# Context halves of batch 0 added by DMA, and the last denominators of a batch copied out of PSUM before they are inverted

## The chip, the cores and the metric

The kernel runs on one core of a Trainium2 chip as one launch. The time is the device time of that core in microseconds. A core has five engines that run their own instruction streams and meet at semaphores: TensorE (PE in the profile, with its weight loads as PEld), VectorE (DVE), ScalarE (ACT), GpSimd (POOL) and SyncE (SP), which here only issues DMAs. [...]

## The reference

Two layers over an fp32 tensor x of 4 batches, 1024 channels and 32 x 32 positions. The change lies in the first, an attention over the N = 1024 positions of each batch:

```python
qkv = (x @ w_qkv.T + b_qkv).reshape(B, N, 3, nh, hd)   # 16 heads of 64
q, k = rmsnorm(rope(q)), rmsnorm(rope(k))
attn = softmax(einsum('bqhd,bkhd->bhqk', q, k) * hd ** -0.5)
ctx  = einsum('bhqk,bkhd->bqhd', attn, v).reshape(B, N, inner)
out  = rmsnorm(ctx @ w_proj.T) + x
```

The second layer is a bottleneck of three convolutions (1x1, 3x3, 1x1) with batch norms, a residual and relu. It is not touched.

## The kernel before, in words

**Stages.** The four batches are worked one after the other: projections of q, k and v, attention, output projection; then the second layer for all batches. The projections are block products of the Strassen kind, in two levels of 7 products each (`OUTER` has the order; `project2` issues them): a PE product of 8 matmuls goes into one PSUM bank, and VectorE, ScalarE and GpSimd make the sums of operands before it and of results after it. The sums of the weights' blocks don't depend on the batch. They are made once, in batch 0: `prepare` (L386-397) and `prepare_blocks` (L399-414) load four blocks, let VectorE make four sums of 128x512 (L392-395), and let GpSimd write them to DRAM (L397, L414), from where later products read them.

A second copy of the program, with shifted scores, stands behind a branch that these inputs don't take.

**Attention.** Each batch has two query halves (`c`, 512 queries each) and eight pairs of heads (`hp`); one step of the two loops is called a head here, 16 a batch. A head has

- eight key tiles `t`: score matmuls for two heads of 64 and two halves of the keys into an `sc` tile (two PSUM banks; three such tiles), L787; the exponential by ScalarE from there into SBUF, 128x1024, L794; and the running sum of the exponentials on VectorE, the denominators `d_` (L798, L800);
- 64 context matmuls (L807) with the values as weights, the lower half of the keys into `o[:, 0]`, the upper half into `o[:, 1]`. `o` is the tile `cx`, of which PSUM has one (two banks);
- the halves' sum: ScalarE copies `o[:, 0]` into its place in `q_all` (L812), and VectorE adds `o[:, 1]` to it (L836). Between the two in VectorE's stream stand what lies in the code between L812 and L835: the multiplication of earlier contexts by their inverse denominators (`mean_of_v`, L764, with GpSimd's bias after it, L765), the inversion of earlier denominators, and in batch 0 one or two weight steps (`extra`: 21 in all).

After every second head, matmuls with ones (L846) sum the denominators over partitions into `dn`, an `sc` tile. In batches 1 to 3 this holds for the second query half alone; the denominators of the first go through `halve` and `sum_of_eight`. What is to be done with `dn` is put on the list `late` and taken from there at the start of the next head, or, for the last one of a batch, 0.1 products into the output projection. That is the function `inverses`: it copies `dn` to SBUF (L900), sends it through DRAM into a small tile `few` of 128x16 (`to_few`, L881-888), inverts it there (L904), sends it back and lets `spread` load it over the partitions (L914). The last `dn` of a batch is treated in another way: VectorE inverts it straight from PSUM, 128x512 (L896), and `spread` copies from SBUF.

**Pools.** `temp` gives tiles of 128x512 in SBUF, four in turn; the weight sets of `prepare` take four each of the eight tiles of `wring`. Attention's PSUM (`sc` 3 x 2 banks, `cx` 1 x 2) and the projections' (`o1` and `o2`, 4 banks each) are the same eight banks: `psum_for` closes the one pools and opens the others, so a projection's first products wait until what lay in their banks has been read.

**Order.** The streams of PE, GpSimd, VectorE and ScalarE follow the code's order here (`manual_schedule`); SP's DMAs are ordered by the framework's scheduler. During a projection `after(n, step)` puts a step n products later; `waiting` holds work that is slipped in when there is room. At the end of a batch's attention the output projection starts with products of q's blocks, while `after(0.1)` issues the last inversion, `after(1)` and `after(4)` the sums of context blocks (L281-284), and `after(3)` the last `mean_of_v`. `load_parts` issues the loads of the next weight set, at the fourth key tile of a head.

Of the kernel before, what the change touches and what calls it, by code (L numbers as in the profile page):

```python
# [13 lines left out]
ALU = mybir.AluOpType  # L14
# [9 lines left out]
NHP = C // (2 * HD)  # L24
CH = 512
NCH = N // CH
# [37 lines left out]
QH = P // 4  # L64
# [21 lines left out]
def program(ctx, tc, x, wblk, w2, w3, vecs, cos, sin, out, bad):  # L86


    nc = tc.nc
# [63 lines left out]
    dens = dram.tile([P, CH], F32, name=f"dens{u}")  # L153
# [4 lines left out]
    with tc.tile_pool(name=f"st{u}", bufs=2) as st, ExitStack() as s:  # L158
# [44 lines left out]
        def bank(kind, name):  # L203
            pool, shape = psum[kind]
            return pool.tile(shape, F32, tag=kind, name=name)

        def temp(name):
            return tmp.tile([P, CH], F32, tag="tmp", name=name)
# [58 lines left out]
        def next_waiting():  # L267
            cost, step = waiting.popleft()
            spend(cost)
            step()  # L270
# [471 lines left out]
        def shifts(q_all, k_all, n, hp, c):  # L742

            rows = []
            for j in range(2):
                d = slice(j * HD, (j + 1) * HD)
                row = temp(f"row_{n}_{j}")[0:1, :]
                for t in range(CH // P):
                    sc = bank("sc", f"sm_{n}_{j}_{t}")
                    q = q_all[d, hp, c * CH + t * P : c * CH + (t + 1) * P]  # L750
                    for kh in range(N // CH):
                        nc.tensor.matmul(sc[:, kh], q, k_all[d, hp, half[kh]], start=True, stop=True)
                    m = acc.tile([P, 1], F32, tag="m", name=f"m_{n}_{j}_{t}")
                    nc.vector.tensor_reduce(m, sc.rearrange("p a k -> p (a k)"), AX.X, ALU.max, negate=True)
                    o = bank("sc", f"mt_{n}_{j}_{t}")[:, 0]
                    nc.tensor.matmul(o[0:1, :P], m, ident, start=True, stop=True)
                    nc.vector.tensor_copy(row[:, t * P : (t + 1) * P], o[0:1, :P])
                rows.append(row)
            return rows
# [7 lines left out]
        def attention(b, c, q_all, k_all, v, probs_, late, ready, extra, slow, steps_in_all, load_parts, fold):  # L767


            at = half[c]  # L770
            sums_, contexts = [], []
            for hp in range(NHP):
                n = f"{b}_{c}_{hp}"
                if late:
                    late.pop(0)()
                rows = shifts(q_all, k_all, n, hp, c) if bad is None else None
                probs = []
                if fold and hp % 2 == 0:
                    d_ = fold[hp // 4][:, hp % 4 // 2 * 2 : hp % 4 // 2 * 2 + 2, :]
                else:  # L780
                    d_ = acc.tile([P, 2, CH], F32, tag="tot", name=f"den_{n}")
                for t in range(N // P):
                    p = probs_[:, t]
                    sc = bank("sc", f"sc_{n}_{t}")
                    for keys in (low, high):
                        for j, d in enumerate((low, high)):
                            nc.tensor.matmul(  # L787
                                sc[keys, j], k_all[d, hp, t * P + keys.start : t * P + keys.stop], q_all[d, hp, at],
                                start=True, stop=bad is not None,
                            )  # L790
                    if bad is None:
                        for j in range(2):
                            nc.tensor.matmul(sc[:, j], ones[0:1, :], rows[j], start=False, stop=True)
                    nc.scalar.activation(p, sc, AF.Exp)  # L794
                    if t == 3:
                        load_parts()
                    if t == 1:
                        nc.vector.tensor_tensor(d_, probs[0], p, ALU.add)  # L798
                    elif t > 1:
                        nc.vector.tensor_tensor(d_, d_, p, ALU.add)  # L800
                    probs.append(p)
                o = bank("cx", f"cx_{n}")
                for t in range(N // P):
                    for j in range(2):
                        h0 = (2 * hp + j) * HD
                        for i, keys in enumerate((low, high)):
                            nc.tensor.matmul(  # L807
                                o[j * HD : (j + 1) * HD, i], v[keys, t, h0 : h0 + HD], probs[t][keys, j],
                                start=(t == 0), stop=(t == N // P - 1),
                            )  # L810

                nc.scalar.copy(q_all[:, hp, at], o[:, 0])  # L812
                contexts.append((q_all[:, hp, at], o[:, 1]))
                sums_.append(d_)
                if hp % 2 == 1:
                    for r in ready:
                        mean_of_v(q_all, *r)
                    ready.clear()
                if fold:
                    halve(hp, d_, fold[hp // 4][:, hp % 4 // 2 * 2 : hp % 4 // 2 * 2 + 2, :])  # L820
                    if hp % 4 == 3:
                        eights.append((hp + 2, lambda n=n, hp=hp: sum_of_eight(b, n, hp, fold[hp // 4], ready)))
                if half_done and half_done[0][0] <= c * NHP + hp:
                    half_done.pop(0)[1]()
                if slow:
                    slow.pop(0)()

                if waiting:
                    next_waiting()
                slots = NCH * NHP - 1  # L830
                if extra and steps_in_all == 0 and hp > 0:
                    extra.pop(0)()
                for _ in range(len(extra) - -(-steps_in_all * max(slots - 1 - c * NHP - hp, 0) // slots) if steps_in_all else 0):
                    extra.pop(0)()
                for cx, other in contexts:  # L835
                    nc.vector.tensor_tensor(cx, cx, other, ALU.add)  # L836
                contexts.clear()
                if eights and eights[0][0] <= c * NHP + hp:
                    eights.pop(0)[1]()
                if hp % 2 == 0 or fold:  # L840
                    continue
                dn = bank("sc", f"dn_{n}")[:, 0]
                for i, d_ in enumerate(sums_):
                    for j in range(2):
                        q = slice((2 * i + j) * QH, (2 * i + j + 1) * QH)
                        nc.tensor.matmul(dn[q, :], ones[:, :QH], d_[:, j], start=True, stop=True)  # L846
                sums_ = []
                late.append(lambda *a, n=n, hp=hp, dn=dn: inverses(b, c, hp, n, dn, ready))

        half_done, eights = [], []  # L850
# [39 lines left out]
        def inverses(b, c, hp, n, dn, ready):  # L890


            r = temp(f"rec_{n}")
            k = 2 * ((b * NCH + c) * NHP + hp - 1)
            if (c, hp) == (NCH - 1, NHP - 1):
                nc.vector.reciprocal(r, dn)  # L896
                nc.sync.dma_start(dens[k : k + 4, :], r[::QH, :])
                spread(c, hp, n, ready, [r[q * QH : (q + 1) * QH, :] for q in range(4)])
                return
            nc.scalar.copy(r, dn)  # L900
            few, rows = to_few(n, k, 4, r[::QH, :])

            def invert():
                nc.vector.reciprocal(few, few)  # L904
                nc.sync.dma_start(rows, few)
                spread(c, hp, n, ready, [dens[k + q, :].partition_broadcast(QH) for q in range(4)])

            half_done.append((0, invert))

        def spread(c, hp, n, ready, rows):  # L910
            w = big_temp(f"inv_{n}")
            for i in range(2):
                for j in range(4):
                    nc.sync.dma_start(w[j * QH : (j + 1) * QH, half[i]], rows[2 * i + j // 2])  # L914
                ready.append((c, hp - 1 + i, w[:, half[i]]))
# [253 lines left out]
        for b in range(B):  # L1169
            units = units_of(room)  # L1170
            q_all = kv.tile([P, NT, N], F32, tag="q", name=f"q_{b}")
# [43 lines left out]
            def load_parts():  # L1215

                while todo and len(made) < 2:
                    made.append(todo.pop(0)(pieces, nc.sync))
# [3 lines left out]
            late, ready, steps_in_all = [], [], len(extra)  # L1222
# [275 lines left out]
        for b in range(B):  # L1498
# [34 lines left out]
            if b == 0 and bad is not None:  # L1533
                o = ps.tile([P, CH], F32, tag="mm", name="fit")
# [20 lines left out]
        for f in range(NT):  # L1555
# [8 lines left out]
            for i, k in order:  # L1564
                b, c = divmod(i, NCH)
# [14 lines left out]
            sc, sh = norms[f] = norm_of(stats, col("g3", f), col("be3", f), f"3_{f}")  # L1580
# [81 lines left out]
```

## Time and profile before

| | |
|---|---|
| time, median of 3 runs | 2700.87 us (2698.98 to 2702.51) |
| profiled execution | 2704.24 us, span 2702.4 us, clock 0.992 |
| busy: PE, DVE, ACT, POOL | 98%, 80%, 41%, 17% of the span |
| attention of batch 0 | 288.3 to 542.2 us |
| its exponentials, L794 | 1.044 us each |
| its denominators, L800 and L798 | 1.225 and 1.217 us each |
| its halves' adds, L836 | 16 of 0.68 us |
| its copies of a half, L812 | 16 of 0.586 us |
| inversions of `few`, L904 | 7 of 0.25 us |
| weight stores by GpSimd, L397 | 68, of 0.55 us to issue each |

A line of the timeline gives start and length in us, the engine, the line, the operation with the tile written and those read, and the count; in brackets the idle time before it and who ended it. Consecutive instructions of one kind are merged. A line of the waits says "engine tile line <- releaser: us in total, times, longest". The stretches are in us from the span's start. A DMA on "SPq" or "POOLq" is shown where it is issued.

### The profile page before, as it was taken

The numbers are of one execution on the slowest core, as the hardware profiler recorded it, in microseconds if no ns is written. First come the engines' busy times: TensorE is split into PE (matmuls) and PEld (weight loads), VectorE is DVE, ScalarE is ACT, GpSimd is POOL, SyncE is SP. The second block draws the span as 40 slices with busy tenths as digits, with TensorE's granted clock in tenths as the row PEclk, the third lists the DMA queues.
The fourth block names the chain that finished last, engine by engine and source line by source line (L and its number), as shares of the span: only waits on it lengthen the run. The fifth ranks groups of instructions, "written<-read, shape, count | busy, mean of one in ns | idle before, by whom it ended". The sixth has DMA issues, their size and how long they took to land. (4 is left out here: it accounts for less than half of the span.)

```text
span 2702.4 us, 40776 instructions
## 1 busy us (share of the span) xinstructions
PE 2642.7 (98%) x15434; PEld 1634.4 (60%) x15434; DVE 2152.2 (80%) x2602; ACT 1112.0 (41%) x1549; POOL 470.0 (17%) x573
## 2 busy tenths in 40 slices
PE   9999998989999999999999999999999999999997
PEld 4448432378888433488887333788884334846843
DVE  5668987988887876887888777788878779877987
ACT  2222454523343565333343556233435554312266
POOL 2542233311011121200011222100111222010000
PEclk9999999999999999999999999999999999999999
DMA  7887665666677453357676441565774443493165
GB/s 274 291 249 220 199 221 190 214 204 194 207 199 207 101 96 70 124 152 222 174 196 175 91 80 41 187 190 181 199 205 106 80 103 121 141 275 123 63 226 210
DMA packets 255661, 459.76 MB, mean 170 GB/s; under 512 B 34912, under 2 KB 127632, under 8 KB 255456
## 3 DMA queue, kind: packets, MB, share of 16 engines
q1 hardware_dynamic: 210528, 306.73, 36.0%
q0 software_dynamic: 44928, 150.33, 22.1%
q8 instruction: 125, 2.05, 0.3%
q14 instruction: 80, 0.66, 0.1%
HBM read 327.43 MB, written 97.01 MB: 157 GB/s over the span
## 5 line engine op out<-in xcount | busy, mean ns | idle before, releaser
L794 ACT ACTIVATE p<-sc 128x1024 f32<-128x1024 f32 x512 | 476.1, 1044 | 18.3 <-PE sc L787 18.2
L787 PE MATMUL sc<-q,k 64*64 64x512 f32 x4096 | 453.1, 591 | 0.0
L800 DVE TENSOR_TENSOR den<-den,p 128x1024 f32<-128x1024 f32 x312 | 385.6, 1236 | 32.9 <-ACT p L794 0.5
L807 PE MATMUL cx<-p,to 64*64 64x512 f32 x3072 | 338.2, 589 | 0.0
L787 PEld LDWEIGHTS sc<-q,k 64*64 64x64 f32 x4096 | 151.0, 132 | 291.7 <-ACT p L794 143.5
L807 PEld LDWEIGHTS cx<-p,to 64*64 64x64 f32 x3072 | 117.4, 133 | 212.2 <-issue 211.9
L485 PE MATMUL p_y<-q,w_y 128*128 128x256 f32 x928 | 217.2, 388 | 21.6 <-issue 21.6
L485 PEld LDWEIGHTS p_y<-q,w_y 128*128 128x128 f32 x928 | 180.3, 195 | 51.3 <-issue 26.1
L480 PE MATMUL p_v<-w_v,x 128*128 128x256 f32 x928 | 210.0, 379 | 0.3 <-DVE x L451 0.2
L765 POOL TENSOR_SCALAR q<-q,vec 128x512 f32<-128x512 f32 x64 | 126.7, 1989 | 393.2 <-DVE q L764 393.2
L480 PEld LDWEIGHTS p_v<-w_v,x 128*128 128x128 f32 x928 | 176.1, 190 | 25.6 <-DVE x L451 1.3
L812 ACT COPY q<-cx 128x512 f32<-128x512 f32 x64 | 37.5, 586 | 362.5 <-PE cx L807 362.5
L485 PE MATMUL p_q<-to,w_q 128*128 128x256 f32 x672 | 152.2, 379 | 0.0
L485 PE MATMUL p_k<-to,w_k 128*128 128x256 f32 x672 | 152.2, 379 | 0.0
L485 PEld LDWEIGHTS p_q<-to,w_q 128*128 128x128 f32 x672 | 127.4, 190 | 18.4 <-issue 1.2
L485 PEld LDWEIGHTS p_k<-to,w_k 128*128 128x128 f32 x672 | 127.4, 190 | 18.4 <-issue 1.2
L807 PE MATMUL cx<-p,rq 64*64 64x512 f32 x1024 | 117.7, 610 | 9.3 <-DVE q L836 9.3
L1566 PE MATMUL c<-h,w 128*128 128x512 f32 x256 | 110.3, 592 | 0.5 <-ACT h L1469 0.5
L798 DVE TENSOR_TENSOR den<-p 128x1024 f32<-128x1024 f32 x52 | 63.5, 1222 | 50.8 <-ACT p L794 50.8
L800 DVE TENSOR_TENSOR den_T<-den_T,p 128x1024 f32<-128x1024 f32 x72 | 88.2, 1225 | 7.9 <-ACT p L794 0.5
L727 POOL DMA_DIRECT2D k<-ks x64 | 57.9, 1096 | 192.4 <-ACT p L794 71.1
L807 PEld LDWEIGHTS cx<-p,rq 64*64 64x64 f32 x1024 | 39.5, 137 | 85.8 <-issue 69.9
(491 smaller groups left out, 4371.7 us busy)
## 6 DMA issues: line engine op xcount, KB each, us to landing
w_v<-wd2f SPq DMA_DIRECT2D x112, 256.0 KB
w_y<-wd2f SPq DMA_DIRECT2D x112, 256.0 KB
w_q<-wd2f SPq DMA_DIRECT2D x84, 256.0 KB
w_k<-wd2f SPq DMA_DIRECT2D x84, 256.0 KB
wd2f<-w_pre POOLq DMA_DIRECT2D x68, 256.0 KB, 4.1
x<-in_x_dram SPq DMA_DIRECT2D x64, 256.0 KB
q<-qs POOLq DMA_DIRECT2D x64, 256.0 KB, 5.5
k<-ks POOLq DMA_DIRECT2D x64, 256.0 KB, 4.5
```

What stands on the lines that cost most here:

```text
L480: nc.tensor.matmul(o[:, q].rearrange("p (g f) -> p g f", g=2), r[:, i, q * P : (q + 1) * P], wt[:, :, i, :], skip_group_check=True, **at,)
L485: nc.tensor.matmul(o[:, q], wt[:, q, i, :], r[:, i, :], skip_group_check=True, **at)
L727: nc.gpsimd.dma_start(dst[i::2, f, :], other[1 - i :: 2, :], accum_op=ALU.add)
L765: nc.gpsimd.tensor_scalar(cx, cx, col("bv", hp), None, ALU.add)
L787: nc.tensor.matmul(sc[keys, j], k_all[d, hp, t * P + keys.start : t * P + keys.stop], q_all[d, hp, at], start=True, stop=bad is not None,)
L794: nc.scalar.activation(p, sc, AF.Exp)
L798: nc.vector.tensor_tensor(d_, probs[0], p, ALU.add)
L800: nc.vector.tensor_tensor(d_, d_, p, ALU.add)
L807: nc.tensor.matmul(o[j * HD : (j + 1) * HD, i], v[keys, t, h0 : h0 + HD], probs[t][keys, j], start=(t == 0), stop=(t == N // P - 1),)
L812: nc.scalar.copy(q_all[:, hp, at], o[:, 0])
L1566: nc.tensor.matmul(os[i], w3t[k][f // NH][:, f % NH, :], h2[b, k][:, half[c]], start=(k == 0), stop=(k == NPT - 1),)
```

## The change

In batch 0, for every head but the last, ScalarE copies both halves out of PSUM, the second into a temporary tile, and GpSimd issues a DMA that adds the one to the other in SBUF (256 KB). The other heads keep VectorE's add, at the same place. For the last denominators of each batch, ScalarE copies `dn` into a temporary tile right after its matmuls; at the place where the inversion was, VectorE inverts the copy in place, and the two transfers after it are the same. In batch 0 one `sc` tile is skipped before the last `dn`.

```diff
@@ attention @@
-                nc.scalar.copy(q_all[:, hp, at], o[:, 0])
-                contexts.append((q_all[:, hp, at], o[:, 1]))
+                cx = q_all[:, hp, at]
+                nc.scalar.copy(cx, o[:, 0])
+                if b == 0 and (c, hp) != (NCH - 1, NHP - 1):
+                    other = temp(f"cx_{n}")
+                    nc.scalar.copy(other, o[:, 1])
+                    nc.gpsimd.dma_start(cx, other, accum_op=ALU.add)
+                else:
+                    contexts.append((cx, o[:, 1]))
...
-                for cx, other in contexts:
-                    nc.vector.tensor_tensor(cx, cx, other, ALU.add)
-                contexts.clear()
+                if contexts:
+                    nc.vector.tensor_tensor(contexts[0][0], *contexts.pop(0), ALU.add)
...
+                if (b, c, hp) == (0, NCH - 1, NHP - 1):
+                    bank("sc", f"skip_{n}")
                 dn = bank("sc", f"dn_{n}")[:, 0]
...
+                if (c, hp) == (NCH - 1, NHP - 1):
+                    r = temp(f"rec_{n}")
+                    nc.scalar.copy(r, dn)
+                    late.append(lambda n=n, hp=hp, r=r: last_inverses(b, c, hp, n, r, ready))
+                    continue
                 late.append(lambda *a, n=n, hp=hp, dn=dn: inverses(b, c, hp, n, dn, ready))
@@ inverses @@
-            if (c, hp) == (NCH - 1, NHP - 1):
-                nc.vector.reciprocal(r, dn)
-                nc.sync.dma_start(dens[k : k + 4, :], r[::QH, :])
-                spread(c, hp, n, ready, [r[q * QH : (q + 1) * QH, :] for q in range(4)])
-                return
             nc.scalar.copy(r, dn)
@@ new @@
+        def last_inverses(b, c, hp, n, r, ready):
+            k = 2 * ((b * NCH + c) * NHP + hp - 1)
+            nc.vector.reciprocal(r, r)
+            nc.sync.dma_start(dens[k : k + 4, :], r[::QH, :])
+            spread(c, hp, n, ready, [r[q * QH : (q + 1) * QH, :] for q in range(4)])
```

## The prediction

> **What bounds the kernel now.** First the page's busy shares:
>
> ```profile
> PE 2642.7 (98%) x15434; PEld 1634.4 (60%) x15434; DVE 2152.2 (80%) x2602; ACT 1112.0 (41%) x1549; POOL 470.0 (17%) x573
> ```
>
> TensorE is the bound over the whole span, so only what shortens a stretch in which TensorE stands still, or runs at a lower clock, can pay. Two places belong to the change: batch 0's attention and the end of each batch's attention. The busy times by stretch (length, then each engine's busy time, clock, DMA share, GB/s):
>
> ```profile
> 288.30:542.20 253.90, 240.46 (x2113) 79.38 (x2112) 222.89 (x239) 133.83 (x152) 77.44 (x106) 0.98 0.63 202
> 1126.60:1130.00 3.40, 3.33 (x8) 2.74 (x9) 3.29 (x3) 0.00 (x0) 0.00 (x0) 0.51 0.73 245
> ```
>
> In the first stretch (batch 0's 16 heads) PE is idle for 13.4 us and VectorE is 88% busy; batches 1 to 3 take 13.73 us a head here with PE 100% busy, so 16 heads would be 220. The second is one outer product after a boundary, at clock 0.51. The view of waits, from 285 to 545, says who PE waits for in batch 0:
>
> ```profile
> DVE few L904 <- DMA few<-densf: 17.9, 7, 5.7
> PEld cx L807 <- DVE q L836: 15.7, 8, 5.3
> PE cx L807 <- DVE q L836: 9.3, 4, 4.4
> PEld dn L846 <- DVE den L800: 8.3, 6, 1.9
> PE dn L846 <- DVE den L800: 4.1, 4, 1.0
> ```
>
> PE waits 9.3 us for the add of the halves (it frees the one context slot in PSUM) and 4.1 us for denominators: both say that VectorE is late. VectorE itself waits 17.9 us, and only for the little tile of denominators. The timeline of one pair shows why:
>
> ```profile
> 409.23 0.59 ACT L900 COPY rec<-dn 128x512 f32<-128x512 f32 x1 [0.63 <-PE dn L846]
> ...
> 415.42 5.64 SPq L383 DMA_DIRECT2D w_pre<-in_wblk_dram  x4
> ...
> 421.16 1.99 SPq L383 DMA_DIRECT2D w_pre<-wdf  x4
> ...
> 423.25 0.50 SPq L883 DMA_DIRECT2D densf<-rec  x1
> ...
> 427.84 0.34 SPq L887 DMA_DIRECT2D few<-densf  x1
> ...
> 430.93 0.25 DVE L904 RECIPROCAL few<-few 128x16 f32<-128x16 f32 x1 [5.72 <-DMA few<-densf]
> ...
> 433.82 0.68 DVE L836 TENSOR_TENSOR q<-q,cx 128x512 f32<-128x512 f32 x1
> ...
> 434.56 10.01 PE L807 MATMUL cx<-p,rq 64*64 64x512 f32 x64 [4.45 <-DVE q L836]
> ```
>
> The denominators are in SBUF at 409.8, but their store leaves at 423.25, behind eight weight loads in SP's queue, which wait for VectorE to free their slots. VectorE idles 5.7 us at L904, then does a weight step and only then L836; PE loses 4.45 us and its context then takes 10.01 us instead of 7.1, because the clock has fallen. Last, the boundary of batch 1:
>
> ```profile
> 1120.02 1.99 PE L485 MATMUL p_y<-q,w_y 128*128 128x256 f32 x8
> ...
> 1123.22 3.35 DVE L896 RECIPROCAL rec<-dn 128x512 f32<-128x512 f32 x1
> ...
> 1126.67 3.58 PE L485 MATMUL p_y<-q,w_y 128*128 128x256 f32 x8 [4.67 <-issue]
> ...
> 1130.09 3.62 PE L485 MATMUL p_y<-y,w_y 128*128 128x256 f32 x16
> ```
>
> The second output product starts 0.1 us after VectorE's reciprocal ends: its PSUM bank lies where `dn` was, and the reciprocal reads `dn` there. It stalls 4.67 us, then takes 3.4 where others take 1.73. The other boundaries look alike; in batch 0 the last `dn` ends at 542.19, the reciprocal at 549.18, the first two products start at 549.27 and the third at 554.69.
>
> [...] here L393 takes 0.98 while L765 runs beside it and 0.69 otherwise[...]
>
> **The change, part by part.**
>
> *Boundaries, four times.* The product that waited for the reciprocal now waits for a 128x512 copy by ScalarE (0.59, as L900). The bank is free at about `dn`'s end + 0.13 + 0.6, with 0.1 to start.
> Batch 0: start at 543.1 (542.19 + 0.9), two products at full clock, third product at 543.1 + 2 x 1.73 = 546.55 instead of 554.69: 8.1. Its sums of q end on VectorE at 545.83, in time.
> Batch 1: the second product follows the first at 1121.75, the third starts at 1123.47 instead of 1130.09: 6.6; its sums end at 1123.3, just in time. Batches 2 and 3 have the same pattern: 6.6 and 6.9. Sum 28.2.
> VectorE's order is kept: the reciprocal still starts at 1123.22 and stays 3.35. So PE is now ahead of VectorE by the gain. Next late in batch 1: VectorE's adds end at 1131.25, then L506, the next sums at about 1134.4, then L764 (1135.7), POOL's L765 pair (4.1, to about 1139.5) and L282, which a product at about 1142.7 needs: some 2 us to spare. If this cover is gone, up to 3 us a boundary go back, 12 in all.
> SP's order at the boundary also moves: two loads of w_y ahead, seven x loads instead of ten up front. Each load issues in about 0.5; the weights that come earlier are needed sooner than the x loads. I take nothing, bounds -2 to +2.
>
> *Batch 0's halves.* 15 adds of 0.68 leave VectorE: 10.2 us. The context slot is freed by two ACT copies, the second 0.59 after the first, so it no longer waits behind a weight step (2.8) and an inverse. ScalarE gains 15 x 0.59 = 8.8 on 134 busy in 254: hidden, except where its copies delay the first exponential of the next head. In odd heads this sits 0.27 after the copy, so it comes about 0.3 later: 8 x 0.3 = 2.4.
> POOL gets 15 issues. The nearest row is the accumulating k<-ks of L727: 1.1 mean to issue, 4.5 to land; the store of a weight block takes 0.55. I take 1.0, bounds 0.55 and 1.8. POOL is 30% busy there (77.4 of 254), so 15 us fit, but the issue stands ahead of that head's L765 and weight stores and waits itself for ACT's copy. They leave 1 to 2.5 us later (ACT's second copy would end at 445.8 in the pair above, where L765 now starts at 444.40; then the issue). Queued behind them: the next weight set, loaded only after a store, and VectorE's step for it. Before, a set whose stores left by 354.4 had its loads issued by 359.2 and was used at 366.6; with a landing like the stores' 4.1 that leaves some 3 us of slack. The data move of 256 KB lands by estimate within 5.5 (the q<-qs row); its reader, L764, comes a pair later, about 28 us. Hidden; without this cover it would be 5 a pair.
> SP's order changes most (the framework's scheduler sets it, and it comes out differently): the store and reload of each pair's denominators stand ahead of the four or eight weight loads. `few` then lands some 5 to 8 us after the pair's end, and VectorE asks for it 12 or more after: most of the 17.9 goes.
>
> *The sum in batch 0.* Pairs started at 288.3, 319.3, 348.3, 380.3, 409.1, 445.5, 480.0 and 511.0, with `dn`'s end at 542.2: 28.9 to 36.4 each. Unstalled, a pair is 6.92 + 6.87 + 6.87 + 6.97 for its matmuls and 1.0 for `dn`, 28.6. Walking VectorE along (9.12 for a head's denominators, 2.8 a weight step, 1.3 an L764 pair, no L836, no wait for `few`), it is at most 5 us behind PE, at which no `dn` waits: 29.0 a pair with the 0.3 for ACT. Batch 0 would end at 521.5 instead of 542.2: 20.7. For weight sets that land late in heads 4, 8 and 10, I take off 2: 18.5.
> Bounds: if the wait for `few` stays, only the 10.2 of VectorE and the slot's wait help, about 9; without late sets, 20.7.
>
> 28.2 + 18.5 = 46.7. Span 2702.4 - 46.7 = 2655.7; that execution took 2704.24 (1.84 around the span), so 2657.5; it lies 3.4 over the median of 2700.87, which gives 2654.2.
>
> **Rivals.**
> *The weight chain takes over (chance 0.2).* POOL's later stores delay loads, VectorE waits for sets instead of `few`; attention gains 0 to 9. For: weight loads are at VectorE's head of queue, and now stand behind the denominators on SP. Against: the 3 us of slack. 2654 + 9.5 to 18.5 gives 2664 to 2673.
> *The boundary gives part back (0.1).* VectorE's remaining reciprocal becomes late for the sums or L764: 12 back, 2666.
> *Slower (0.07).* The accumulating DMA heads POOL's in-order queue, waits for the context's end there, and holds L765 and four weight stores until then. If stores leave 7.6 us later in each of 15 heads, 3.3 are slack and 4.3 reach VectorE and then PE: 15 x 4.3 = 65 against 46.7 gained, so 2719. It decides from some 6.4 us of delay a head (15 x 3.1 = 46.7). Against: the worst I find is the 2.5 above.
> *Nothing gained at the boundary (0.01).* If the product's real wait is on something that ended with the reciprocal by chance, 28.2 is missing: 2682; four boundaries with the same 0.1 us after it speak against. This also is where no change could come from, with the second rival's zero.
>
> **How the numbers follow.** Both parts hold: 0.62, 2654, its own range 2649 to 2662 (a microsecond or two at each boundary, up to 5 of late sets). With the two rivals of 2664 to 2673 at 0.3, the range for 8 in 10 is 2646 to 2676: the low end is the 2.2 taken off for late sets, the 2 at SP's boundaries and the 3.5 by which the runs shown spread (2654.2 - 7.7). 0.2%, 5.4 us, is about what a measurement can tell from no change: faster 0.92, same 0.01, slower 0.07.
>
> **What would show it.** Right: no idle PE over 1 us after the boundaries, the product after them at 1.7 to 1.9; no `L904` wait over 1 us; no PE wait for VectorE in `cx`; batch 0's heads at 14.5 us; accumulating DMAs landing in 3 to 6. Wrong: waits of VectorE for w_pre or of POOL for ACT's second copy, heads of over 15 us, PE waits on L764 or L765 in the output projection, or a reciprocal still just ahead of a product.

## The result and the profile after

The changed kernel takes 2666.45 us (median of 4 runs, 2663.41 to 2667.97) against 2701.69 of the kernel before beside it: ratio 0.9869, 95% interval 0.9851 to 0.9886. That is 35.2 us less, where 46.7 were forecast; the time lies inside the forecast's range, above the likeliest case's own. Measured once more later, beside another 11 runs of the kernel before, it was 2663.83 (0.9853, 0.984 to 0.9865).

The page's busy shares of the changed kernel, and the busy times of batch 0's attention (length, PE, PEld, DVE, ACT, POOL with their counts, clock, DMA share, GB/s):

```profile
PE 2630.3 (99%) x15434; PEld 1627.9 (61%) x15434; DVE 2144.5 (80%) x2587; ACT 1121.1 (42%) x1568; POOL 480.9 (18%) x588
...
289.00:525.60 236.60, 234.11 (x2113) 77.82 (x2112) 215.82 (x225) 140.21 (x167) 87.59 (x121) 1.00 0.76 229
```

The attention of batch 0 has shrunk from 253.9 to 236.6 us; VectorE is busy 7.1 us less, and PE is idle for 2.5 us instead of 13.4. Its waits over the whole span, from the view of waits (us in total, times, longest):

```profile
PE p_y L485 <- DMA w_y<-wdf: 4.5, 4, 2.3
PE dn L853 <- DVE den L800: 2.5, 4, 1.0
PE p_q L485 <- DMA w_q<-wdf: 2.1, 1, 2.1
...
PE p_v L480 <- DMA w_v<-wdf: 1.4, 1, 1.4
PE p_v L480 <- DVE x L451: 1.3, 2, 1.0
```

The kernel before has this line in the same view, for the four stalls after the attentions:

```profile
PE p_y L485 <- issue: 21.6, 4, 7.1
```

These 21.6 us are gone (0.7 is left), and so is the 9.3 us for the context slot. New is the first line of the changed kernel's: each output projection waits once for weights. The pair of batch 0 that answers to the one shown of before, in the timeline:

```profile
408.13 0.50 SPq L895 DMA_DIRECT2D densf<-rec  x1
...
410.37 0.34 SPq L899 DMA_DIRECT2D few<-densf  x1
...
415.80 4.30 SPq L383 DMA_DIRECT2D w_pre<-in_wblk_dram  x4
...
422.25 0.25 DVE L911 RECIPROCAL few<-few 128x16 f32<-128x16 f32 x1
...
422.79 0.90 POOL L817 DMA_DIRECT2D q<-cx  x1 [6.39 <-ACT cx L816]
...
428.04 7.05 PE L807 MATMUL cx<-p,rq 64*64 64x512 f32 x64
```

The store of the denominators now leaves at 408.13, ahead of the weight loads instead of behind them; VectorE inverts `few` without waiting, and the context runs at full clock (1.00 over its 7.05 us, against 0.71 over the 10.01 us of the kernel before). The boundary of batch 1, in the timeline:

```profile
1098.22 1.06 PE L853 MATMUL dn<-den,ones 128*32 128x512 f32 x8
1099.22 3.72 PE L485 MATMUL p_y<-q,w_y 128*128 128x256 f32 x16
1102.42 3.35 DVE L919 RECIPROCAL rec<-rec 128x512 f32<-128x512 f32 x1
1102.78 3.62 PE L485 MATMUL p_y<-y,w_y 128*128 128x256 f32 x16
1105.80 0.51 SPq L920 DMA_DIRECT2D densf<-rec  x1
1106.35 5.00 SPq L927 DMA_DIRECT2D inv<-rec  x8
1111.45 2.59 SPq L472 DMA_DIRECT2D w_y<-wd2f  x3
...
1114.61 0.93 SPq L383 DMA_DIRECT2D w_y<-wdf  x2
...
1119.35 1.99 PE L485 MATMUL p_y<-to,w_y 128*128 128x256 f32 x8 [0.87 <-DMA w_y<-wdf]
```

The second product no longer waits for the reciprocal, and runs at full clock (1.00 from 1099.22 to 1106.00). But SP's queue stands still from 1103.77 until the reciprocal ends at 1105.77, then spends 5 us on eight copies, and only then issues the weights. They arrive 0.87 us late.

Laying the two timelines side by side, matmul by matmul (the start of each in the one less that in the other), gives the whole account. PE's lead grows by 16.55 us up to batch 0's last `dn` (17.3 of it within the attention, which began 0.8 later). The boundaries of batches 0 to 3 bring 8.24, 6.52, 7.93 and 6.78, together 29.5. Given back are 0.80, 1.04, 0.84 and 2.51 at the first product with `to` of each, 5.2 in all, then 3.2 in batch 1's q projection, 1.3 in batch 2's v projection and 0.2 elsewhere. 16.55 + 29.5 - 5.2 - 3.2 - 1.3 - 0.2 = 36.2, and the spans differ by 36.2. (The expectations below were written with 29.2 and 5.0 for the second and the third of these.)

### The profile page after: what moved, and what is told of

Its sections match the earlier page's. It is cut to its first block, busy times and chain, and to the rows that moved or that the text cites. A ratio compares the mean times of both kernels' runs of the same rounds, so it can differ in the third digit from the quotient of the medians.

```text
span 2666.2 us, 40828 instructions
## 1 busy us (share of the span) xinstructions
PE 2630.3 (99%) x15434; PEld 1627.9 (61%) x15434; DVE 2144.5 (80%) x2587; ACT 1121.1 (42%) x1568; POOL 480.9 (18%) x588
## 5 line engine op out<-in xcount | busy, mean ns | idle before, releaser
L485 PE MATMUL p_y<-q,w_y 128*128 128x256 f32 x928 | 209.8, 379 | 0.7 <-issue 0.7
L485 PE MATMUL p_y<-to,w_y 128*128 128x256 f32 x384 | 90.5, 380 | 4.5 <-DMA w_y<-wdf 4.5
L480 PE MATMUL p_v<-w_v,t 128*128 128x256 f32 x384 | 90.1, 379 | 1.4 <-DMA w_v<-wdf 1.4
```

The source lines that it names most:

```text
L480: nc.tensor.matmul(o[:, q].rearrange("p (g f) -> p g f", g=2), r[:, i, q * P : (q + 1) * P], wt[:, :, i, :], skip_group_check=True, **at,)
L485: nc.tensor.matmul(o[:, q], wt[:, q, i, :], r[:, i, :], skip_group_check=True, **at)
```

## The experiments

**The two parts alone.** First the last denominators without the halves, VectorE adding from PSUM as before:

```diff
-                if b == 0 and (c, hp) != (NCH - 1, NHP - 1):
-                    other = temp(f"cx_{n}")
-                    nc.scalar.copy(other, o[:, 1])
-                    nc.gpsimd.dma_start(cx, other, accum_op=ALU.add)
-                else:
-                    contexts.append((cx, o[:, 1]))
+                contexts.append((cx, o[:, 1]))
```

> Only the last denominators are changed, batch 0's halves are added by VectorE as before. Theory (the two parts add up; at the boundary the bank comes free with ScalarE's copy): batch 0's attention stays at 254 us from its first score to the last dn; the stalls of 4.7 to 7.1 us after each dn are gone and 29 us are gained there; the waits for w_y of 0.6 to 2.4 us at the first product with to, 5.0 us in all, are there as in the changed kernel. Time 2701.7 - 29.2 + 5.0 = 2677.5, or 2682 if the later waits in batch 1's q and batch 2's v projection (4.4 us) also come from this part. Rival (the boundaries' gain needs the shorter attention, or its order of loads): under 15 us gained, 2687 or more.

Measured: 2676.51 against 2700.98, ratio 0.9904 (0.9888 to 0.9921): 24.5 us. Three boundaries bring what they brought together; batch 0's brings 6.6 instead of 8.2, because its first products ran at a lower clock (0.57 from 538.4 to 541.5). The wait for w_y is there (2.6 us, three times). Batch 0's attention took 250.6 us in this trace; its code and the order of SP's issues are those of before there, so 250.6 and 253.9 show that this stage can vary by 3 us between executions.

Then the halves without the last denominators (the last `dn` inverted from PSUM):

```diff
+            if (c, hp) == (NCH - 1, NHP - 1):
+                nc.vector.reciprocal(r, dn)
+                nc.sync.dma_start(dens[k : k + 4, :], r[::QH, :])
+                spread(c, hp, n, ready, [r[q * QH : (q + 1) * QH, :] for q in range(4)])
+                return
...
```

> Only batch 0's halves are changed; the last denominators are inverted from PSUM as before. Theory: batch 0's attention takes 236 to 238 us instead of 254, the four boundaries stall as before, no wait for w_y in them: 2701.7 - 17.3 = 2684.4. Rival (the attention's gain is given back where PE arrives earlier): 2690 or more.

Measured: 2689.37, ratio 0.9949 (0.9933 to 0.9966): 11.6 us, less than the 17.3 expected, with an attention of 238.2 and the four stalls as before. The 17.3 was read between two traces, and the one of before ran 3.4 us over its kernel's median. 24.5 + 11.6 = 36.1 against 35.2 for both: the parts add up.

**Which half of the halves?** Using the DMA also changed SP's order. So the kernel before got that order and nothing else:

```diff
+                with tc.manual_schedule(engines={mybir.EngineType.SP if b == 0 else mybir.EngineType.PE}):
                 attention(
...
```

> The kernel before with one thing changed: in batch 0's attention SP's transfers go in the order in which they are written, which puts the store and reload of each pair's denominators ahead of the next weight loads, as in the changed kernel; nothing else moves. Theory (the wait for few is a large part of VectorE's lag): VectorE's 17.9 us of waiting for few fall below 3, batch 0's attention takes 242 to 247 us: 2690 to 2695. Rival (VectorE's load by the adds, and the slot in PSUM that they hold, are what counts): attention 251 to 254, time 2699 to 2702.

Measured: 2687.72, ratio 0.9947 (0.993 to 0.9963): 13.3 us, no less than the DMAs with the order brought. The attention took 235.7 us, better than the theory's 242 to 247. Its waits of PE, from 285 to 530, are one line; VectorE waits for no `few`:

```profile
PE dn L846 <- DVE den L800: 1.0, 1, 1.0
```

VectorE still does all 16 adds from PSUM here. The opposite test is the changed kernel with the old order, the denominators' transfers behind the weight loads:

```diff
                     if t == 3:
                         load_parts()
+                        while sends:
+                            sends.pop(0)()
...
-            few, rows = to_few(n, k, 4, r[::QH, :])
+            sends.append(lambda: sent.append(to_few(n, k, 4, r[::QH, :])))
...
```

> The changed kernel with the store and reload of each pair's denominators behind the weight loads again, in SP's order of the kernel before. Theory (the wait for few counts): VectorE waits 10 us or more for few, batch 0's attention takes 242 to 248 us instead of 236.6, time 2672 to 2678. Rival (the adds count alone): attention within 2 us of 236.6, time 2666 to 2669.

Measured: 2678.55, ratio 0.9908 (0.9891 to 0.9925), just beyond the theory's end. The attention took 253.1 us, more than its 248, and the time is 2.0 above that of the first run, which has SP's old order too but no DMAs: without the order the DMAs gain nothing. From its views of waits of PE and of VectorE, 285 to 545, and its timeline:

```profile
PE dn L855 <- DVE den L802: 12.7, 6, 6.5
```

```profile
DVE few L917 <- DMA few<-densf: 20.3, 6, 8.2
```

```profile
432.42 0.25 DVE L917 RECIPROCAL few<-few 128x16 f32<-128x16 f32 x1 [8.16 <-DMA few<-densf]
...
444.56 1.92 PE L855 MATMUL dn<-den,ones 128*32 128x512 f32 x4 [6.54 <-DVE den L802]
```

The context no longer waits for VectorE, since ScalarE frees the slot. But VectorE idles 8.16 us for `few`, the next head's denominators are late too, and PE now loses 12.7 us at `dn` where it lost 9.3 at `cx` and 4.1 at `dn`. And the time that the adds freed on VectorE became idle time: it is busy for 215.0 of these 253.1 us, idle for 38.1 where it was idle for 31.0 before. Of the 7.1 more, 2.4 are waits for `few` (20.3 instead of 17.9), 3.0 for exponentials and 1.3 for weight sets.

Last, the changed kernel without its DMAs, in its SP order (the edit of the first run and that of the third together; in the traces SP's issues from 286 to 545 follow one another as in the changed kernel, transfer by transfer):

> The changed kernel without its accumulating DMAs: VectorE adds the halves from PSUM as in the kernel before, while SP's transfers stand in exactly the order of the changed kernel. New theory (the attention's gain is SP's order alone): batch 0's attention 235 to 238 us, time 2664 to 2669. The prediction's reading (VectorE's 15 adds and the slot they held are part of the gain): 241 to 246 us, 2671 to 2677.

Measured: 2664.42, ratio 0.986 (0.9844 to 0.9877), attention 236.4 us:

```profile
289.60:526.00 236.40, 235.17 (x2113) 78.89 (x2112) 222.48 (x240) 133.83 (x152) 77.37 (x106) 1.00 0.68 217
```

VectorE is busy 222.5 us here against 215.8 in the changed kernel, and the stage is no longer: PE is idle 1.2 us in it. Once more, with the changed kernel beside it in five rounds:

> The changed kernel once more, on the same chip as the run beside it: 2664 to 2668.

> The changed kernel without its accumulating DMAs and in its SP order, once more beside it. Theory (the DMAs add nothing to the gain): within 3 us of the changed kernel, on either side. Rival (they bring part of the 10.2 us of VectorE's adds): 4 us or more above it.

The changed kernel took 2663.83 (0.9853, 0.984 to 0.9865), the one without DMAs 2662.34 (0.9849, 0.9836 to 0.9862). They can't be told apart: the median without the DMAs was the lower one, by 1.5 us here and by 2.0 between 2664.42 and the first 2666.45, where the rival wanted it 4 us higher.

So four kernels, all with the last denominators changed, differ in these two things alone: in SP's old order 2676.51 without the DMAs and 2678.55 with them, in the new order 2664.42 and 2666.45. The order is worth 12.1 us either way. The 2.0 us that the DMAs seem to cost is inside the intervals. The trace of the changed kernel has a sign of such a cost: VectorE waits for weight sets, from the view of waits between 285 and 530,

```profile
DVE w_pre L392 <- DMA w_pre<-in_wblk_dram: 4.4, 2, 2.2
...
DVE w_pre L392 <- DMA w_pre<-wdf: 1.0, 2, 0.7
```

against 0.7 us without the DMAs. Whether the sets are late because GpSimd issues and stores later, or because the DMA share is 0.76 instead of 0.68, was not separated.

**The skipped tile.** The changed kernel without it:

```diff
-                if (b, c, hp) == (0, NCH - 1, NHP - 1):
-                    bank("sc", f"skip_{n}")
```

> The changed kernel without the skipped sc tile ahead of batch 0's last dn. Theory: dn then lies under other banks of the output projection, but a copy of 0.6 us frees it before the second product asks for it, as in batches 1 to 3: the first product starts 0.1 to 0.2 us after dn instead of 0.73, time within 1 us of the changed kernel. Rival: the bank is one that the first product needs, and the wait of 0.7 stays or grows to 2.

One execution: 2667.19, and the first product waits 0.73 us with and without it. The theory of the wait missed; the tile makes no difference that one execution can show.

**What holds w_y back.** The reading from the timeline was SP's queue. So the eight copies and the store went to ScalarE's queue:

```diff
-            nc.sync.dma_start(dens[k : k + 4, :], r[::QH, :])
-            spread(c, hp, n, ready, [r[q * QH : (q + 1) * QH, :] for q in range(4)])
+            def send():
+                spread(c, hp, n, ready, [r[q * QH : (q + 1) * QH, :] for q in range(4)], nc.scalar)
+                nc.scalar.dma_start(dens[k : k + 4, :], r[::QH, :])
+
+            after(1.5, send)
...
```

> The changed kernel, but the nine transfers of each batch's last inverses (eight copies over the partitions, one store) are issued from ScalarE's queue, 1.5 products into the output projection, instead of SP's. Theory (the loads of w_y are late because SP's queue holds them behind the reciprocal and 5 us of issues): no wait of PE for w_y over 0.3 us at the first product with to, 5.0 us in all gained, 2661.5. Rival (the loads are late because the ring's slots come free late, or by landing): the waits stay, 2665 to 2668. Against both: ScalarE's copies of p_y are held for some 4 us behind its issues; if the banks ran out, PE would wait for ScalarE there, and the time would be over 2668.

Measured: 2689.87, ratio 0.9955 (0.9939 to 0.9972), 23 us worse than the changed kernel. Its timeline:

```profile
1111.21 8.35 ACTq L931 DMA_DIRECT2D inv<-rec  x8
...
1122.15 2.07 PE L485 MATMUL p_y<-y,w_y 128*128 128x256 f32 x4 [4.39 <-ACT y L574]
```

From the first of the eight issues to the end of the last 8.35 us passed, and behind them stood ScalarE's copies that free the products' banks; PE waited 19.6 us for them in all. The issues themselves are no slower than SP's. From the views of line L927 of the changed kernel and of line L931 here (ns: shortest, median, longest), and from the views of DMAs of both (size, median us to landing):

```profile
L927 SPq DMA_DIRECT2D inv<-rec x32: 507/588/605, 533.2 to 2250.3; - x32
```

```profile
L931 ACTq DMA_DIRECT2D inv<-rec x32: 514/515/625, 534.1 to 2271.3; - x32
```

```profile
inv<-rec SPq DMA_DIRECT2D x32, 64.0 KB, 2.0
```

```profile
inv<-rec ACTq DMA_DIRECT2D x32, 64.0 KB, 6.5
```

The rest of the 8.35 us (some 4.2, with eight issues of 0.515) is waiting for landings. In the trace's semaphores each issue waits for the one that it will raise itself. On SP the eight have eight of them; on ScalarE they share four, and the fifth issue, which takes up the first's again, starts at 1116.80, right after the first copy has landed at 1116.78. PE no longer waited for w_y, but arrived so much later that this says nothing. The combination with SP's order and without DMAs,

> SP's order of the changed kernel, the last denominators copied by ScalarE, their transfers on ScalarE's queue, and no accumulating DMA. Theory: the sum of the two runs beside it, attention 236 us and no wait for w_y: 2660 to 2663, below the changed kernel. Rival: one of the two costs what the other gains, 2666 or more.

took 2684.71 (0.9938, 0.9921 to 0.9954), some 20 more than without ScalarE's issues: the rival, by the same stall.

In none of these traces does PE wait for GpSimd there. On the kernel without accumulating DMAs, its queue was given the same nine transfers (`nc.gpsimd` in place of `nc.scalar`, right behind the reciprocal):

> The kernel without accumulating DMAs, in SP's order of the changed kernel, and with the transfers of each batch's last inverses issued from GpSimd's queue instead of SP's. Theory (SP's queue holds the loads of w_y back, and GpSimd, unlike ScalarE, has nothing at that time that PE waits for): no wait for w_y over 0.3 us at the first product with to, some 4 to 5 us gained on 2664.4: 2659 to 2661. Rival 1 (ring slots or landing make the loads late): waits stay, 2664. Rival 2 (eight issues on GpSimd take 8 us or more, so the last contexts' inverses come late and PE waits for L282 later on): 2665 to 2675.

Measured: 2663.09 (0.9858, 0.9844 to 0.9872), no gain on 2662.34 of the run beside it. The eight issues took 4.04 us, without gaps. SP issued the two loads that are waited for at 1105.26 and 1106.98, 6.9 and 5.2 us before PE asks for them at 1112.13, and yet:

```profile
1113.42 1.99 PE L485 MATMUL p_y<-to,w_y 128*128 128x256 f32 x8 [1.29 <-DMA w_y<-wdf]
```

The busy times by stretch show why, first of this run, then of the changed kernel at the same places, 6.3 us later by the clock (the last two numbers are DMA share and GB/s; the view's share can come out a little above 1):

```profile
1104.00:1108.00 4.00, 4.00 (x20) 3.54 (x19) 3.79 (x7) 0.12 (x1) 0.34 (x1) 1.00 0.94 294
1108.00:1112.00 4.00, 4.00 (x20) 3.29 (x18) 1.94 (x3) 1.17 (x2) 2.63 (x2) 1.00 1.07 332
```

```profile
1110.00:1114.00 4.00, 4.00 (x21) 3.51 (x19) 3.97 (x7) 0.47 (x1) 0.00 (x0) 1.00 0.50 133
1114.00:1118.00 4.00, 4.00 (x20) 3.53 (x19) 3.06 (x4) 1.17 (x2) 3.65 (x2) 1.00 0.85 252
```

With SP's queue free, the x loads of the next batch go out early too, and the DMA engines are full (share 0.94 and 1.07). In the changed kernel they stand half idle while SP is held (0.50 from 1110 to 1114). So the queue was one reason, and by this reading not the only one. The last run delays the x loads and, with SP in written order, puts loads of w_y ahead of them:

```diff
-                    after(3 + 1.5 * j, load)
+                    after(9 + 1.5 * j, load)
...
-                    after(3 + 1.5 * (2 * i + 3) + 2, queue)
+                    after(9 + 1.5 * (2 * i + 3) + 2, queue)
...
+            with tc.manual_schedule(engines={mybir.EngineType.SP if b + 1 < B else mybir.EngineType.PE}):
             ty = qk_proj(b, WP, q_all, tc_, None, yt[b], "y", None, two)
```

> The kernel without accumulating DMAs and with the last inverses' transfers on GpSimd's queue, and now with the next batch's x loaded later in batches 0 to 2: from the ninth instead of the third unit of the output projection on, and behind the w_y loads of the sets that are due before (SP in written order during the projection). Theory (in the run without this, the DMA engines were 94 to 107% busy from 4 us after dn on, and w_y landed over 6 us after its issue: the x loads take the bandwidth): no wait over 0.3 us for w_y at the first product with to in batches 0 to 2, DMA share in that stretch below 0.8, and 2 to 3 us less, 2660 to 2661, unless the sums of x, now later, make the q projection wait. Rival (w_y is late for another reason): waits of 0.8 to 1.3 us a batch stay.

Measured: 2663.69 (0.9853, 0.9837 to 0.9869). Its stretch before the first product with `to`, and its waits of PE over the span:

```profile
1109.00:1113.00 4.00, 4.00 (x21) 3.51 (x20) 2.81 (x4) 1.17 (x2) 3.75 (x2) 1.00 0.64 150
```

```profile
PE p_q L485 <- ACT q L539: 3.2, 3, 1.1
PE p_y L485 <- DMA w_y<-in_wblk_dram: 1.7, 2, 1.0
...
PE p_y L485 <- DMA w_y<-wdf: 1.2, 1, 1.2
```

The DMA share is 0.64 there (0.83 and 0.85 in the 8 us before it), and the wait for `w_y<-wdf` is left in batch 3 alone, whose loads were not moved. So it is the x loads that made w_y late in the run before it, by their place in the queue or by the bandwidth they take: the run moved both. The gain that the theory named does not come: later loads of w_y and the next q projection now wait, 4.9 us together.

## Why the prediction was right or wrong

*Boundaries: right in mechanism and size.* 28.2 forecast, 29.5 measured (8.2, 6.5, 7.9, 6.8 against 8.1, 6.6, 6.6, 6.9). The run with this part alone shows that it stands by itself. The reciprocal takes 3.34 us from the copy (L919) and 3.35 from PSUM (L896), in the median of four each: the 3.35 that the author estimated for the copy holds.

*What is late next at a boundary: wrong.* The step named VectorE's chain from the reciprocal to L282, with 2 us to spare; that chain held, and PE waited for none of it. The step that failed is SP's order at the boundary, "I take nothing, bounds -2 to +2": 5.2 us went back there. In batch 1 PE comes 6.5 us earlier, while the two loads of w_y that it waits for are issued only 3.5 and 4.7 us earlier, measured from the reciprocal. They stand behind the eight copies in SP's queue, and the step did not count this. The runs with the queue freed and the x loads moved say that the queue is not the only limit, and curing it did not pay.

*Given back in later projections: not forecast.* 3.2 us in batch 1's q projection and 1.3 in batch 2's v projection. The first is a wait for `w_q<-wdf`, 1.7 us longer than before, and a product behind it that ran at a mean clock of 0.57. The wait was 0.4 in the kernel before, 2.1, 1.7, 1.6 and 1.5 in the four traces that have the DMAs, the new order and the last denominators changed (two of the changed kernel, one without the skipped tile, one with ScalarE's queue), and 0.7 or less in those that have the last two without the DMAs. So it goes with the DMAs; by what path was not tested. This and the 5.2 make up the miss between the two traces, but for 2.0 less in the attention and 1.3 more at the boundaries.

*Batch 0's attention: near in size, wrong in cause.* 18.5 forecast, 16.6 on PE's clock (17.3 in length) between the two traces; by their medians the run with this part alone and that with its order alone gained 11.6 and 13.3. The trace of before, on which the forecast rests too, ran 3.4 us over its kernel's median. The sum built the gain from three things at once, the 10.2 us of adds, the slot, and the wait for `few`. The runs give all of it to the last, through SP's order: 235.7 us with the order alone, 253.1 with the DMAs in the old order. The bound "if the wait for `few` stays, about 9" was the wrong step: it is 0.8 on the traces, and nothing by the times. It treated VectorE's freed time as time gained. But VectorE was waiting for a transfer further on in the chain, so the removed work became idle time (38.1 us with the DMAs in the old order, 31.0 before), and the lag came out at `dn` (12.7 us of PE's waits). With `few` early, VectorE's lag no longer reaches PE, and its 222.5 us of work fit into 236.4. That the sum with three causes came out near its size was luck in so far as two of them bring nothing. (Its last step is also off by 1.2: eight pairs of 29.0 from 288.3 end at 520.3, not at 521.5.)

*What held the store back: read wrongly in part.* The prediction says that the loads ahead of the store wait for VectorE to free their slots. SP's own waits in the kernel before, from 288 to 542, name GpSimd's stores of the sets before, which have to land first (they come after VectorE's step):

```profile
SPq L383 <- DMA wd2f<-w_pre: 78.6, 34, 11.6
```

*ScalarE's second copy: no cost seen on PE.* 2.4 us were charged for later exponentials. The second pair took 28.63 us (319.43 to 348.06), as fast as the unstalled pair of the forecast.

*GpSimd: right but for the landing's bound.* 0.89 us to issue (1.0 forecast), 3.9 to land in the median but up to 6.6 (5.5 at most forecast), the readers a pair later. Weight sets did land late, 5.4 us on VectorE instead of the 2 taken off; most of it stayed off PE's path, where 2.5 us of waits for `dn` are left.

*The rivals.* "The boundary gives part back" named 2666 and its time came out, but by the weights and not by VectorE. "The weight chain takes over" named 2664 to 2673, which holds the measured time too, but with 0 to 9 us gained in the attention, which gained more: the time alone would have spoken for either. The slower rival needed 6.4 us of delay a head; nothing of that size appeared. Of the signs of being wrong that the prediction lists, one came, VectorE's waits for `w_pre`; of those of being right, one did not hold: PE idled for up to 2.3 us after a boundary.

## What to carry to other kernels

When an edit lets the framework's scheduler reorder a queue, test the order by itself: here 14 small transfers placed ahead of the weight loads were the whole gain of a part whose visible edit, moving adds off the busiest helper engine, brought nothing. Work taken from an engine that waits for something else can become idle time, as here (38.1 us of it instead of 31.0), so follow what the engine waits for before pricing what it does. When the bound engine arrives earlier, list what it meets there: here the loads kept their place behind eight copies, and with the queue freed the DMA engines were full (share 0.94 to 1.07). And when a row of DMA issues takes long, see whether it is the issues or the landings they wait for.

## What the runs showed of the hardware that was not expected

*Issuing a DMA.* The same copy within SBUF (32x512) took 0.51 to 0.61 us to issue on SP (the changed kernel), 0.51 to 0.63 on ScalarE and 0.50 to 0.58 on GpSimd (the two runs with their queues). The eight of batch 1's boundary took 5.00 us on SP and 4.04 on GpSimd, but 8.35 on ScalarE, where the later ones waited for earlier ones to land, and ScalarE's copies stood behind them (PE waited 19.6 us for those in all).

*Landing.* These copies of 64 KB landed in 2.0 us in the median from SP's queue, with the DMA share at 0.50 to 0.64 around those of batch 1, and in 6.5 from ScalarE's and 6.8 from GpSimd's, with the share at 0.94 to 1.07 from the issue of GpSimd's in batch 1 on (1100 to 1112). A load of w_y issued 5.2 us before PE asked for it still came 1.29 us late where the share was 0.94 to 1.07.

*The clock.* In the changed kernel the product behind an idle time of 2.09 us ran at a mean clock of 0.57; the one behind 2.35 us of idle time (at 2259.89, in batch 3's output projection) ran at 1.00. From its timeline, and its busy times over the product behind the first of these waits:

```profile
658.15 3.38 PE L485 MATMUL p_q<-t,w_q 128*128 128x256 f32 x8 [2.09 <-DMA w_q<-wdf]
```

```profile
658.15:661.30 3.15, 3.15 (x8) 2.52 (x9) 2.94 (x5) 0.00 (x0) 1.77 (x4) 0.57 0.70 269
```
